# Down stage of a Strassen feed-forward: two sets of PSUM banks, left operands in three steps, the next rows' norm in half steps

## The chip, the cores and the metric

One core of one Trainium2 chip. The metric is the device time of one execution in microseconds, the median of three runs.

## What is computed

Rows `x` are 2 x 2048 rows of 1024 values, all float32. Cut to what matters, the reference is:

```python
x = x + attention(layernorm(x))            # one head of 256, then Wo and bo
n = layernorm(x)                           # no gain, no bias
h = relu(n @ up_w) ** 2                    # 1024 -> 2048
shared = h @ down_w                        # 2048 -> 1024
rw = sum of the two largest of n @ gate_w  # 8 gates
routed = ((n @ fc1_w) @ expert_w * rw) @ fc2_w      # 1024 -> 512 -> 512 -> 1024
x = x + layernorm(shared + routed) * ln_gamma + ln_beta
```

The change lies in the second product of the feed-forward, `h @ down_w` together with the routed part: the down stage.

## The kernel before

The attention comes first (lines 406 to 759) and writes its rows to DRAM (`x1`). Then the feed-forward runs over four pairs of row blocks (`for b in range(NBB)`, line 999). A pair is 2 x 512 rows. Each b has an up stage (line 1061) and a down stage (line 1165). Instructions of this part stand in the order in which they are written (`manual_schedule`, line 998); the attention ahead of it is ordered by a scheduler.

**Matmuls.** Every float32 operand is split into a high and a low half that the matmul can take (`hi` a copy, `lo` the difference). A product of two such operands is three matmuls (`Pass3`, line 117). A matmul here is 128x128 by 128x512 and fills one PSUM bank.

**Products.** Both stages use a Strassen-like scheme: seven products of quarters instead of eight. The down stage takes them in the order p1, p2, p6, p5, p3, p7, p4. A product has 10 pieces of the inner dimension (k, `NK`), and for each piece four row tiles (t, `NB`): 12 matmuls per k, 120 per product, 840 per stage. Each product sums its four row tiles in four banks (`accs`, line 1167). p2, p3 and p4 go on adding to the banks of the product before them (`a.more()`, line 1170), after that one's sums have been copied or added into `y` (lines 1212 to 1229: on ScalarE, called ACT, for p1 and p2, on VectorE, called DVE, for the others). `acc_bank` (line 840) hands out banks of two pools, `psb` (2 banks) and `psa` (4), in a rotation of six. The pool `psc` (2 banks) isn't used by the down stage.

**Right operands (w).** `next_piece` (line 827) keeps three pieces ready. In each call it ends one piece, starts loads until two are under way, and casts one. For a raw piece the cast is on ACT (line 813) and the difference on DVE (line 821). A finished piece is written to DRAM by the POOL queue (line 824, `w_p<-w`), so that later b load both halves at once (line 793). All loads of w are on the SP queue (lines 793 and 796). b=0 has all pieces raw and stores those of even i, b=1 has those of odd i raw and stores them, b=2 and b=3 only load. There are seven w buffers.

**Left operands (sp).** `cast_s` (line 1024) does the Strassen sum of h on DVE, where a product has one (p2 line 1035, p6 line 1029, p5 line 1033), and casts the result on ACT (line 1039). `end_s` (line 1042) takes the difference on DVE (line 1044), and for p6 one more (line 1046). `next_s` (line 1056) keeps two ready. So in the loop at piece k, the difference of piece k+1 is taken, and sum and cast of piece k+2 are issued. There are four sp buffers.

**The norm of the next rows.** `Norm.step` (line 922) works on four tiles of 128 rows of the next pair in a pipeline of 11 steps. A full step issues, in this order: a load of a tile (SP queue), the transpose of a normalised tile on DVE and its write to DRAM (lines 213 and 218, POOL queue, `xt_d<-xblk`), the normalisation of a tile (two small DVE operations, lines 276 and 282, then ACT, line 283), the second moment and the first moment of two tiles (ACT, lines 271 and 259), and the fetch of a transposed tile (line 224, POOL queue, `xt<-xt_d`). Tile t is loaded in step t and goes through first moment, second moment, normalisation, write and fetch 2, 3, 4, 5 and 7 steps later. `norm1` steps at k = 0, 2, 4, 6, 8 of p1 and p2 and at k=0 of p6; `norm2` likewise in p5, p3 and p7 (lines 1182 to 1184). b=3 has no next rows.

**Other work in the down stage.** In p7 and p4 the tiles of norm1 are split for the next up stage (line 1189), and `out_step` (line 974) finishes output rows: a load of `res` (SP), a transfer that adds beta (POOL), moments on ACT, two DVE operations (lines 966 and 967) and the write of the output (POOL).

Of the kernel before, what the change touches and what calls it, by code (L numbers as in the profile page):

```python
# [17 lines left out]
P = 128  # L18
SQ = 32
W = 512  # L20
# [5 lines left out]
def kernel(  # L26
# [33 lines left out]
    NB = W // P  # L60
# [777 lines left out]
    n_bank = [0]  # L838
# [74 lines left out]
    class Norm:  # L913
# [2 lines left out]
        STEPS = NB + 7  # L916

        def __init__(self, n):
            self.n, self.i = n, 0
            self.r, self.m, self.d, self.x = {}, {}, {}, {}  # L920

        def step(self):
            load, first, second, norm, write, fetch = (
                self.i - lag for lag in (0, 2, 3, 4, 5, 7)
            )
            self.i += 1
            if load in range(NB):
                self.r[load] = load_row(x1[self.n][ts(load, P), :])
            if write in range(NB):
                self.d[write] = transpose_write(self.r[write])  # L930
            if norm in range(NB):
                self.m[norm].normalise()
            if second in range(NB):
                self.m[second].second()
            if first in range(NB):
                self.m[first] = Moments(self.r[first], "n")
            if fetch in range(NB):
                self.x[fetch] = fetch_tile(self.d[fetch])

    class Out:  # L940

# [56 lines left out]
    with tc.manual_schedule():  # L998
        for b in range(NBB):
# [19 lines left out]
                "p1": "11", "p2": "12", "p6": None, "p5": "21", "p3": "12", "p7": "11", "p4": "22",  # L1019
            }  # L1020
            todo_s = DOWN[:]
            sp, sp_cast = [], []

            def cast_s(at=None):
                p, k = todo_s.pop(0)
                a11, a12, a21, a22 = (h_at(a, k) for a in ("11", "12", "21", "22"))
                if p == "p6":
                    v = half("s2")
                    add(v, a11, a22, ALU.add)
                else:  # L1030
                    v = h_at(FROM[p], k)
                if p == "p5":
                    add(a21, a21, a22, ALU.subtract)
                elif p == "p2":
                    add(a11, a11, a21, ALU.subtract)
                t = at
                if t is None:
                    t = wp.tile([P, 2 * W], FR, tag="sp", name="sp", bufs=4)
                nc.scalar.copy(t[:, 0:W], v)  # L1039
                sp_cast.append((v, t, a12 if p == "p6" else None))  # L1040

            def end_s():
                v, t, a12 = sp_cast.pop(0)
# [2 lines left out]
                    add(a12, a12, v, ALU.subtract)  # L1046
                sp.append(t)

            def more_s(n):
                while (todo_s or sp_cast) and len(sp) < n:  # L1050
                    if sp_cast:
                        end_s()
                    if todo_s and not sp_cast:
                        cast_s()

            def next_s():
                more_s(2)
                return sp.pop(0)

            rwb, acc = [None, None], {}  # L1060
            for m, (p, i) in enumerate(UP):
                flush()
                w = next_piece()
                if p != "p2":
                    acc[i] = Pass3(acc_bank("pu"), NCC // 2)
                ps = acc[i].ps
                if p == "p2":
                    acc[i].more()
                for c in range(NCC // 2):
                    acc[i].add(piece(w, c, P, slice(0, P)), piece(X[p], c, W, slice(0, W)))  # L1070
                lat, pair = i >= HU // P, i % 2 and i < HU // P
                c22, c21 = h_at("22", i), h_at("21", i) if m >= 2 * NK else None
                if p == "p1":
                    nc.scalar.copy(c22, ps)
                elif p == "p2":
                    if lat:
                        add(h_at("11", i), ps, rwb[0], ALU.mult)
                    else:
                        relu(h_at("11", i), ps)
                        if pair:  # L1080
                            square(h_at("11", i, 2))
                elif p == "p4":
                    nc.scalar.copy(c21, ps)
                elif p == "p6":
                    add(c22, ps, c22, ALU.subtract)
                    add(c21, c21, c22, ALU.subtract)
                elif p == "p5":
                    add(c22, c22, ps, ALU.add)
                elif p == "p3":
                    c12 = h_at("12", i)  # L1090
                    add(c12, c22, ps, ALU.add)  # L1091
                    if lat:
                        add(c12, c12, rwb[0], ALU.mult)
                    elif pair:
                        relu(h_at("12", i, 2), h_at("12", i, 2))
                        square(h_at("12", i, 2))
                else:
                    add(c21, c21, ps, ALU.add)
                    add(c22, c22, ps, ALU.subtract)
                    if lat:  # L1100
                        add(c21, c21, rwb[1], ALU.mult)
                        add(c22, c22, rwb[1], ALU.mult)
                    elif pair:
                        for v in ("21", "22"):
                            relu(h_at(v, i, 2), h_at(v, i, 2))
                            square(h_at(v, i, 2))

                if m % 2 and m < 15:
                    out_step()
                if b == 0 and m in (0, 1, 2, 4, 6, 8, 9, 10, 11, 12, 13):  # L1110
                    norm2.step()

                if m == 12:
                    x_t[1] = norm2.x
                    X["p4"] = new_x()
                if m >= 13 and m % 2 and m < 2 * NK:
                    split_x(x_t[1], 1, (m - 13) // 2, X["p4"], split_late)
                elif m >= 2 * NK and p != "p7":
                    n = {"p4": "p6", "p6": "p5", "p5": "p3", "p3": "p7"}[p]
                    if i == 1:  # L1120
                        X[n] = new_x()
                    if i % 2 and i < 2 * NB:
                        if p == "p4":
                            sums_x(x_t, i // 2)
                        r_, f_ = PLACE[n]
                        split_x(x_t[r_], f_, i // 2, X[n], split_late)

                if m == 0:
                    ga = half("ga")[: 2 * NE, :]
                    nc.scalar.copy(ga, gate_part(X["p1"], 0))  # L1130
                elif m == 2:
                    gs = half("gs")[: 2 * NE, :]
                    add(gs, ga, gate_part(X["p2"], 1), ALU.add)
                    gt = Gate(gs)
                elif (p, i) == ("p4", 1):
                    add(ga, ga, gate_part(X["p4"], 1), ALU.add)
                elif (p, i) == ("p7", 0):
                    add(ga, ga, gate_part(X["p7"], 0), ALU.subtract)
                    gt = Gate(ga)
                if m == 6 or (p, i) == ("p7", 3):  # L1140
                    gt.largest()
                elif m == 10 or (p, i) == ("p7", 6):
                    rwb[p == "p7"] = gt.spread()
                if p == "p7" and i >= NK - 5:
                    if sp_cast:
                        end_s()
                    if len(sp) < 3:
                        cast_s()
            X = {}


# [12 lines left out]
                norm1, norm2 = Norm(2 * b + 2), Norm(2 * b + 3)  # L1164
            for j, p in enumerate(("p1", "p2", "p6", "p5", "p3", "p7", "p4")):
                if p in ("p1", "p6", "p5", "p7"):
                    accs = [Pass3(acc_bank("pd"), NK) for _ in range(NB)]
                else:
                    for a in accs:
                        a.more()  # L1170
# [5 lines left out]
                for k in range(NK - late):  # L1176
# [2 lines left out]
                    for t in range(NB):  # L1179
                        down(t, s, w)  # L1180
                    if more:
                        for m, n in enumerate((norm1, norm2)):
                            if k % 2 == 0 and 3 * m <= j < 3 * m + 3 and n.i < Norm.STEPS:
                                n.step()
                        if j >= 5 and k % 2 and k < 2 * NB:
                            n = "p1" if j == 5 else "p2"
                            if k == 1:
                                X[n] = new_x()
                            split_x(norm1.x, j - 5, k // 2, X[n], split_late)
# [12 lines left out]
                if late:  # L1202
                    last_w = [next_piece() for _ in range(late)]
                    both = unit("last")
                    while len(sp) + len(sp_cast) < late:
                        if sp_cast:
                            end_s()
                        i = len(sp) - late + 2
                        cast_s(both[:, ts(i, 2 * W)] if i >= 0 else None)
                    end_s()  # L1210
                    last = [(sp.pop(0), w) for w in last_w]
                for t in range(NB):
                    for s, w in last if late else ():
# [74 lines left out]
```

## Time and profile before

| | us |
|---|---|
| median of 3 runs | 2413.64 (2413.22 to 2415.35) |
| the profiled execution's own time | 2414.37 |
| its span, first to last instruction | 2412.4 |
| TensorE busy | 2348.1 |
| VectorE (DVE) busy | 1463.5 |
| ScalarE (ACT) busy | 1131.3 |
| POOL busy | 299.5 |

The mean granted TensorE clock is 0.992 of full speed, and DMA moves 250 GB/s on the mean. In the profile, PE is the matmul side of TensorE and PEld its weight loads, which overlap. Matmuls overlap each other too, so a busy PE is not a PE at its peak: the distance from one start to the next tells more than the duration of one. An idle time is put down to the instruction that ended it. A share of busy time is a mean over stages with different limits, and is to be read by stage.

### The profile page before, as it was taken

What the parts mean: (1) busy time and instruction counts of PE and PEld (TensorE: products, weight loads), DVE (VectorE), ACT (ScalarE), POOL (GpSimd) and SP (SyncE); (2) the same over time, 40 slices, a digit from 0 to 9 for tenths busy, and PEclk for the clock granted to TensorE, in tenths of its full rate; (3) what the DMA queues carried; (4) which work ended last, traced back from release to release, by engine and by line L of the source; (5) the groups of instructions that cost most, each with busy time, mean ns of one, the idle gap of its engine ahead of it and who ended that gap; (6) DMA issues with size and microseconds to landing.
All of it is one profiled execution on the core that took longest, in us unless ns stands there. A gap on an engine that the chain in (4) does not pass through costs nothing.

```text
span 2412.4 us, 29279 instructions
## 1 busy us (share of the span) xinstructions
PE 2348.1 (97%) x10704; PEld 1922.9 (80%) x10704; DVE 1463.5 (61%) x2168; ACT 1131.3 (47%) x1846; POOL 299.5 (12%) x450
## 2 busy tenths in 40 slices
PE   8999899999998999999999999999999999999998
PEld 7888778888787778777777877777888887788886
DVE  5566549888777466687736458653446663445545
ACT  5555445555544553666552274544135354314224
POOL 3222110012110010011210011110000010000001
PEclk9999999999999999999999999999999999999999
DMA  5867883999996666677997778897557798655695
GB/s 186 320 245 266 286 201 110 287 317 320 285 244 183 214 230 184 230 244 243 337 307 237 239 265 316 316 333 259 194 184 266 257 325 292 212 194 185 203 310 189
DMA packets 225807, 603.99 MB, mean 250 GB/s; under 512 B 18768, under 2 KB 80720, under 8 KB 223616
## 3 DMA queue, kind: packets, MB, share of 16 engines
q1 hardware_dynamic: 152160, 334.02, 40.5%
q0 software_dynamic: 73504, 268.11, 36.3%
q8 instruction: 85, 1.39, 0.2%
q14 instruction: 58, 0.48, 0.1%
HBM read 448.96 MB, written 210.76 MB: 273 GB/s over the span
## 4 chain that ended last, share of the span: by engine, by line
PE 69%; issue 12%; DVE 6%; DMA 5%; ACT 5%; POOL 2%; POOLq 0%; SPq 0%; ACTq 0%; DVEq 0%
PE pu L130 28%; PE pd L130 21%; PE po L130 6%; PE ps L130 6%; PE pw L130 3%; DMA w<-wt 2%; DVE xblk L213 1%; DMA xres<-in_L_attn_bo_dram 1%; PE pg L870 1%; ACT xrow L283 1%; PE pf L130 1%; PE pq L130 1%; ACT junk L271 1%; DMA w_p<-w 1%; DVE w L821 1%
## 5 line engine op out<-in xcount | busy, mean ns | idle before, releaser
L130 PE MATMUL pd<-w,sp 128*128 128x512 f32 x3336 | 769.6, 392 | 18.8 <-DVE sp L1044 8.7
L130 PEld LDWEIGHTS pd<-w,sp 128*128 128x128 f32 x3336 | 625.8, 188 | 161.5 <-DVE sp L1044 18.0
L130 PE MATMUL pu<-xh,w 128*128 128x512 f32 x2240 | 692.9, 390 | 1.5 <-DVE w L821 0.8
L130 PEld LDWEIGHTS pu<-xh,w 128*128 128x128 f32 x2240 | 419.2, 188 | 92.4 <-DVE w L821 2.3
L130 PE MATMUL pu<-xl,w 128*128 128x512 f32 x1120 | 436.5, 390 | 2.9 <-DVE xl L150 2.8
L130 PEld LDWEIGHTS pu<-xl,w 128*128 128x128 f32 x1120 | 210.2, 188 | 48.3 <-DVE xl L150 4.6
L1044 DVE TENSOR_TENSOR sp<-h,sp 128x512 fp32r<-128x512 f32 x238 | 162.4, 687 | 128.2 <-ACT sp L1039 127.9
L1039 ACT CAST sp<-h 128x512 fp32r<-128x512 f32 x238 | 145.6, 618 | 182.7 <-PE pd L130 132.8
L130 PE MATMUL ps<-q,k 128*128 128x512 f32 x768 | 196.9, 394 | 3.7 <-DVE max L560 3.6
L130 PE MATMUL po<-p,v 128*128 128x512 f32 x768 | 197.2, 396 | 1.2 <-ACT p L142 1.1
L813 ACT CAST w<-w 128x512 fp32r<-128x512 f32 x210 | 128.1, 617 | 149.1 <-DMA w<-wt 140.3
L821 DVE TENSOR_TENSOR w<-w 128x512 fp32r<-128x512 f32 x210 | 142.8, 685 | 88.7 <-ACT w L813 87.0
L130 PEld LDWEIGHTS ps<-q,k 128*128 128x128 f32 x768 | 143.0, 189 | 38.5 <-DVE max L560 9.0
L130 PEld LDWEIGHTS po<-p,v 128*128 128x128 f32 x768 | 144.8, 190 | 31.9 <-ACT p L142 1.5
L824 POOL DMA_DIRECT2D w_p<-w x140 | 75.7, 541 | 586.6 <-DVE w L821 525.9
L992 ACT ACTIVATE h<-h 128x1024 f32<-128x1024 f32 x48 | 50.6, 1055 | 208.0 <-DVE h L1091 159.7
L555 ACT COPY s<-ps 128x512 f32<-128x512 f32 x128 | 75.0, 586 | 152.3 <-PE ps L130 148.9
L150 DVE TENSOR_TENSOR xl<-xt,xh 128x512 fp32r<-128x512 f32 x104 | 71.6, 688 | 120.8 <-ACT xh L149 120.7
L213 DVE STREAM_TRANSPOSE xblk<-xrow 128x1024 f32<-128x1024 f32 x60 | 120.4, 2007 | 39.1 <-ACT xrow L283 36.4
L560 DVE TENSOR_TENSOR max<-ps,max 128x512 f32<-128x512 f32 x120 | 82.4, 687 | 45.2 <-ACT s L555 45.1
L130 PE MATMUL pq<-xha,w_h 128*128 128x512 f32 x256 | 99.7, 389 | 0.0
L130 PE MATMUL pq<-xha,w_l 128*128 128x512 f32 x256 | 99.7, 389 | 0.0
(181 smaller groups left out, 3040.7 us busy)
## 6 DMA issues: line engine op xcount, KB each, us to landing
w<-w_p SPq DMA_DIRECT2D x350, 512.0 KB, 4.3
w_p<-w POOLq DMA_DIRECT2D x140, 512.0 KB, 4.7
w<-wt SPq DMA_DIRECT2D x210, 256.0 KB, 3.6
xt_d<-xblk POOLq DMA_DIRECT2D x56, 512.0 KB, 3.5
xt<-xt_d POOLq DMA_DIRECT2D x56, 512.0 KB, 6.3
wt<-in_L_ffn_up_w_dram POOLq DMA_DIRECT2D x9, 2048.0 KB, 24.9
wt<-in_L_ffn_down_w_dram POOLq DMA_DIRECT2D x9, 2048.0 KB, 34.1
xres<-in_L_attn_x_dram SPq DMA_DIRECT2D x32, 512.0 KB, 12.4
```

The costliest lines, as they stand in the source:

```text
L130: nc.tensor.matmul(self.ps, lhsT=a, rhs=b, start=self.i == 0, stop=self.i == self.n - 1, skip_group_check=self.on,)
L150: late_ops.append(lambda: nc.vector.tensor_tensor(lo, t, f32(hi), ALU.subtract))
L213: nc.vector.transpose(b.rearrange("p (q k i) -> p q k i", q=P // SQ, i=SQ), r.rearrange("p (k i q) -> p q k i", k=NCC, i=SQ),)
L271: nc.scalar.activation(self.junk(), self.v, AF.Square, bias=self.nm, accum_out=s2)
L555: nc.scalar.copy(s["s"][k // 4][:, ts(k % 4, W)], pm)
L560: nc.vector.tensor_tensor(s["max"], pm, s["max"], ALU.max)
L813: nc.scalar.copy(w[:, 0:W], f32(w)[:, W : 2 * W])
L821: nc.vector.tensor_tensor(w[:, W : 2 * W], v[:, W : 2 * W], v[:, 0:W], ALU.subtract)
L824: nc.gpsimd.dma_start(out=kept[key], in_=w.bitcast(FP))
L992: nc.scalar.activation(o, v, AF.Relu)
L1039: nc.scalar.copy(t[:, 0:W], v)
L1044: add(t[:, W : 2 * W], v, f32(t)[:, 0:W], ALU.subtract)
```

## The change

The down stage's banks: p1 with p2, and p5 with p3, take two banks of `psb` and two of `psc`; p6, and p7 with p4, take the four of `psa`. The rotation of `acc_bank` starts anew in each b. Left operands: sum, cast and difference are three steps, `sum_s`, `cast_s` and `end_s`, one k apart, so that at piece k the sum of k+3, the cast of k+2 and the difference of k+1 are issued. The norm: a step falls into two halves, load, transpose with its write and normalisation in the first, second and first moments and the fetch in the second. One half is issued after each of the k = 0 to 7 of p1, p2, p6 (norm1) and p5, p3, p7 (norm2), and none at k = 8 and 9. The number of instructions on ACT, DVE, POOL and SP is the same. SP's order is the same. On POOL, the write of the fourth transposed tile and the fetches of tiles 1 and 2 move from p2 to p6 and from p3 to p7, and the fetch of tile 3 moves from k=0 to k=5 of p6 and p7. On TensorE, the first six matmuls of the first up product now stand among the last ones of the attention.

```diff
-        def step(self):
+        def step(self, halves=(0, 1)):
             load, first, second, norm, write, fetch = (
                 self.i - lag for lag in (0, 2, 3, 4, 5, 7)
             )
-            self.i += 1
-            if load in range(NB):
...
+            if 0 in halves:
+                if load in range(NB):
+                    self.r[load] = load_row(x1[self.n][ts(load, P), :])
+                if write in range(NB):
+                    self.d[write] = transpose_write(self.r[write])
+                if norm in range(NB):
+                    self.m[norm].normalise()
+            if 1 in halves:
+                if second in range(NB):
+                    self.m[second].second()
+                if first in range(NB):
+                    self.m[first] = Moments(self.r[first], "n")
+                if fetch in range(NB):
+                    self.x[fetch] = fetch_tile(self.d[fetch])
+                self.i += 1
+
+        def half_step(self):
+            if self.i < Norm.STEPS:
+                self.step((self.half,))
+                self.half = 1 - self.half
...
-            def cast_s(at=None):
+            def sum_s():
                 p, k = todo_s.pop(0)
...
-                t = at
+                sp_sum.append((v, a12 if p == "p6" else None))
+
+            def cast_s(t=None):
+                v, a12 = sp_sum.pop(0)
                 if t is None:
                     t = wp.tile([P, 2 * W], FR, tag="sp", name="sp", bufs=4)
                 nc.scalar.copy(t[:, 0:W], v)
...
+            def step_s(at=None):
+                if sp_cast:
+                    end_s()
+                if sp_sum:
+                    cast_s(at)
+                if todo_s:
+                    sum_s()
+
             def more_s(n):
-                while (todo_s or sp_cast) and len(sp) < n:
-                    if sp_cast:
-                        end_s()
-                    if todo_s and not sp_cast:
-                        cast_s()
+                while (todo_s or sp_sum or sp_cast) and len(sp) < n:
+                    step_s()
...
+            n_bank[0] = 1
             for m, (p, i) in enumerate(UP):
...
                 if p in ("p1", "p6", "p5", "p7"):
-                    accs = [Pass3(acc_bank("pd"), NK) for _ in range(NB)]
+                    pools = (psb, psb, psc, psc) if p in ("p1", "p5") else (psa,) * 4
+                    accs = [Pass3(bank(q, "pd"), NK) for q in pools]
...
                     if more:
-                        for m, n in enumerate((norm1, norm2)):
-                            if k % 2 == 0 and 3 * m <= j < 3 * m + 3 and n.i < Norm.STEPS:
-                                n.step()
+                        if j < 6 and k < NK - 2:
+                            (norm1, norm2)[j // 3].half_step()
```

Two further places follow from the three steps: the end of the up stage calls `step_s` in each of its last five pieces, and the last product of b=3 prepares its five held-back pieces with `step_s`.

More of the change, by code (lines that the diff above doesn't have):

```diff
@@ L918, in __init__ @@
         def __init__(self, n):
-            self.n, self.i = n, 0
+            self.n, self.i, self.half = n, 0, 0
             self.r, self.m, self.d, self.x = {}, {}, {}, {}
-        def step(self):
+        def step(self, halves=(0, 1)):
             load, first, second, norm, write, fetch = (
@@ L925, in step @@
             )
-            self.i += 1
-            if load in range(NB):
[L928 to L938, printed above, removed]
+            if 0 in halves:
[17 more added lines that the diff above has]
+                self.half = 1 - self.half
     class Out:
@@ L1021 @@
             todo_s = DOWN[:]
-            sp, sp_cast = [], []
-            def cast_s(at=None):
+            sp_sum, sp_cast, sp = [], [], []
+            def sum_s():
                 p, k = todo_s.pop(0)
@@ L1039, in cast_s @@
                 nc.scalar.copy(t[:, 0:W], v)
-                sp_cast.append((v, t, a12 if p == "p6" else None))
+                sp_cast.append((v, t, a12))
             def end_s():
@@ L1144 @@
                 if p == "p7" and i >= NK - 5:
[L1145 to L1148, printed above, removed]
+                    step_s()
             X = {}
@@ L1204 @@
                     both = unit("last")
[L1205 to L1210, printed above, removed]
+                    while len(sp) < late:
+                        i = len(sp) + len(sp_cast) - late + 2
+                        step_s(both[:, ts(i, 2 * W)] if sp_sum and i >= 0 else None)
                     last = [(sp.pop(0), w) for w in last_w]
```

## Prediction

> **What bounds the kernel now.** I first cut the span into stages, since a mean over stages with different limits says nothing on this change. Rows are the four down stages (b = 0 to 3); columns: window, its length, busy time and count per engine, granted clock, DMA share, GB/s.
>
> ```profile
> core 0: us, PE busy (x) PEld busy (x) DVE busy (x) ACT busy (x) POOL busy (x), PEclk, DMA share, GB/s
> 1004.40:1209.90 205.50, 196.14 (x841) 157.39 (x840) 158.22 (x247) 126.47 (x236) 34.84 (x59) 0.99 0.81 275
> 1411.30:1615.90 204.60, 195.62 (x841) 157.77 (x840) 136.88 (x211) 108.31 (x200) 34.75 (x59) 0.99 0.91 320
> 1817.20:2009.00 191.80, 191.35 (x841) 157.21 (x840) 115.92 (x175) 89.77 (x164) 16.17 (x24) 1.00 0.83 288
> 2210.20:2400.70 190.50, 190.50 (x841) 157.48 (x840) 99.98 (x150) 64.85 (x117) 9.71 (x13) 1.00 0.71 235
> ```
>
> All do the same 840 matmuls. b=3 never waits: 190.5/840 = 0.2268 us each, 2.72 us per k (12 matmuls), 27.2 per product. TensorE bounds all four; what can go is the excess: 15.0 + 14.1 + 1.3 = 30.4 us. By products, the windows that aren't 27.2, here of b=0 (p2, p3, p7, p4), and p7 of b=2:
>
> ```profile
> 1034.40:1065.70 31.30, 29.96 (x120) 23.49 (x121) 26.89 (x41) 19.47 (x35) 7.11 (x12) 0.95 0.71 233
> 1120.10:1151.20 31.10, 28.69 (x122) 22.18 (x121) 23.48 (x35) 18.71 (x33) 7.09 (x12) 1.00 0.76 247
> 1151.20:1181.60 30.40, 27.95 (x121) 22.20 (x120) 21.69 (x34) 21.21 (x44) 8.12 (x12) 1.00 1.04 359
> 1181.60:1210.10 28.50, 27.73 (x120) 22.39 (x121) 21.91 (x34) 12.58 (x23) 3.75 (x7) 1.00 0.91 300
> 1954.70:1981.90 27.20, 27.20 (x122) 22.52 (x121) 16.70 (x25) 18.71 (x38) 4.76 (x7) 1.00 1.04 357
> ```
>
> Two kinds: in p2 and p3 no resource is full and DMA is at 0.7; in p7 the DMA share is 1. The matmul timeline says who was late (last bracket):
>
> ```profile
> 1034.45 16.02 PE L130 MATMUL pd<-w,sp 128*128 128x512 f32 x61 [2.44 <-ACT y L1217]
> 1054.76 73.68 PE L130 MATMUL pd<-w,sp 128*128 128x512 f32 x323 [0.97 <-DVE sp L1044]
> 1129.43 0.49 PE L130 MATMUL pd<-w,sp 128*128 128x512 f32 x1 [0.99 <-ACT sp L1039]
> 1181.60 5.92 PE L130 MATMUL pd<-w,sp 128*128 128x512 f32 x25 [1.59 <-ACT sp L1039]
> ```
>
> Summing starts beyond 0.2268 us: p1's end 4.29 (b=0), 1.76 (b=1); p2 from k4 2.37, 2.48, 0.12; p3 3.88, 2.16, 1.40: together **18.46**. p7 and p4: 1.46 + 3.05, 5.43 + 2.40, none: 12.34. Why p2 and p3 wait is in the two queues in one full norm step:
>
> ```profile
> 1042.10 0.69 DVE L821 TENSOR_TENSOR w<-w 128x512 fp32r<-128x512 f32 x1 [2.71 <-ACT w L813]
> 1043.91 1.99 DVE L213 STREAM_TRANSPOSE xblk<-xrow 128x1024 f32<-128x1024 f32 x1
> 1045.97 0.16 DVE L282 TENSOR_TENSOR nb<-nm,rs 128x1 f32<-128x1 f32 x1
> ...
> 1046.17 1.25 ACT L283 ACTIVATE xrow<-xrow,nb,rs 128x1024 f32<-128x1024 f32 x1 [2.54 <-DVE nb L282]
> 1041.46 0.60 ACT L813 CAST w<-w 128x512 fp32r<-128x512 f32 x1
> ```
>
> Each engine idles 2.5 us for the other. DVE needs 4.03 us from its w to nb; ACT from normalise (1037.58) through second and first to the cast of the next w (ends 1042.06) 4.5. That is one closed loop, 8.6 us (nb ends 1037.54 and 1046.13), for two k of 5.44.
>
> **What the Trainium skill says.** PSUM — Partial Sum Buffer, "PSUM bank collisions raise a hardware error": readers and matmuls are to be kept apart by bank. So p2, which adds to p1's banks, waits for the copies; the trace agrees (2.44 us). Same page, "Engine vs sequencer instructions": ScalarE and VectorE queues are strict FIFO; the loop above shows it. TensorE: Matmul & The Clock Gate, "Part 1": an idle stretch halves the clock for some 3.4 us; here at 1034.4, nine starts that were 0.43 us instead of 0.23, 1.7 of the 4.29. DMA: Bandwidth & Descriptors, "Issuing engines are not separate DMA queues": all transfers interleave on 16 engines; p7 agrees, its w loads take 7 to 10 us to land, against 2.6 to 3.4 in p3.
>
> **The change, part by part** (against the profiled execution, 2414.4 us, span 2412.4).
>
> *Half steps, p1's end.* Before, the step at k=8 puts normalise, second and first (3.9 us) ahead of ACT's casts and the four copies of p1. Now the last half is at k=7, and ACT has 2 x 1.04 us of casts in 5.44 us before the copies. Gain 6.05, the clock dip with it.
>
> *Half steps, p2 and p3.* After nb ACT does normalise (1.2) and one cast before DVE may go on: 1.9 + 4.0 = 5.9 us per two k. ACT's own sum is 4 casts x 0.52 + 1.15 + 1.46 + 1.28 = 6.0. Both exceed 5.44, so p2 of b=0 loses 0.5 per full step. I carried both queues through k by k, each instruction at the start-to-start time of the rows above (DVE 0.60, transpose 1.91, reciprocal and nb 0.27; ACT casts 0.52), each waiting for its source. p1's last copy ends 0.8 us into p2; ACT's two casts then end at 1.8, DVE's w and sp at 2.5, for a use at 5.44 (k2): 2.9 early. The same at k4, k5, k6, k7, k8: 2.1, 2.8, 1.4, 2.2, 0.9 early. Two bare k give 0.9 each back. p2 has three transposes instead of four. p3 has no sums (0.6 less per k on DVE): least 0.5. b=1 and b=2 have less to cast. Gain 2.37 + 2.48 + 0.12 + 7.44 = 12.41; I leave 0.5 for the thin places, so **18.0** in all. The cover is those 0.5 to 0.9 us; without it some 0.5 per late k returns.
>
> *Fourth transpose.* It moves to p6 k0 and p7 k0. p6 has DVE at 4 x 0.6 = 2.4 per k, plus 1.9 once: sp is then 1.9 us early at k2 and gains 0.3 per k. p7 k0: the evictions of p3 end 0.9 us into it, then w, sp, transpose, w, sp: ready at 5.3 for k2 at 5.44. Nothing, but barely: the lead built in p3 hides it, and if DVE comes later, all of its delay is lost once, 0.1 to 2 us. Queued behind on DVE are w and sp of the next k, then the low half of a split tile; ACT's casts don't wait for them.
>
> *Three-step operands.* The same adds, casts and subtractions, the add one k earlier, so ACT's cast no longer waits for an add of its own k (63.9 us of idle ACT in 30 waits, which p6 without any stall shows to be off the path). The four sp buffers hold as before: two ready, one cast, one in use. A sum of p6 lives a k longer, three of four half buffers; no norm scratch is asked for then, its last is at k5 of p2. I add nothing beyond the above; if the buffers were short, an add would wait a k, which the sp lead of 1.9 us hides in part: 0.8 us per time.
>
> *Bank sets.* Before, six banks went round, so a product's first two were free and its last two were those that the previous product's first two copies left 1.4 us and more earlier. No matmul in the waits stands for a DVE eviction. Nothing: the matmuls on t0 and t1 hide it. If DVE came late, the new sets would save that, 0.7 us per copy, which no row shows. p1 to p2, p5 to p3, p7 to p4 still share banks. Resetting the rotation lets six matmuls of the first up product be issued among the last attention ones, one of them in a 7.44 us idle of TensorE at the half clock: 0.2 to 0.45, I take **0.3**.
>
> *DMAs that move.* SP's order is unchanged. On POOL, per block, the fourth write of xt_d and the fetches of tiles 1 and 2 go from p3 into p7 (k0, k1, k3), the third fetch from k0 to k5. Behind them wait the stored pieces (w_p), whose landing frees buffers for the next loads, and the beta adds. (For norm1 they go from p2 to p6, where the share is 0.78 to 0.91: room.) 512 KB at p7's 359 GB/s are 1.46 us, so 4.4 us of DMA time come into a product that has none free. Pairing each load with its matmuls, the time from landing to use sinks to 7.0 us in p7 of b=0 and to 1.0 at k3 of p4 in b=2. But two of the three were issued at p3's end and landed 8 to 10 us later, already among the traffic of p7; the share was 0.7 to 0.95 just before. So only what becomes idle there is lost: I estimate 2 us per block, not shown by the trace. b=0 and b=1 already stall and pay it; b=2 pays what exceeds 1.0, say 0.5: **+4.5**. Bounds: 4.4 x 3 - 1.0 = +12.2; below nothing, -6, if w_p, no longer behind a fetch that waits 4 us for its write, frees loads sooner.
>
> Sum: 2414.4 - 18.0 - 0.3 + 4.5 = 2400.6; the median of the runs is 0.7 under the profiled one: **2399.9**. With 2 us either way on the gain and 4 on the DMAs, 2394 to 2405.
>
> **Rivals.**
> - *The moved DMAs cost all they can* (+12.2): 2407.6. For: b=2's 1.0 us. Against: part was there already. 0.17.
> - *The loop only moves*: half of the 18 stays since 5.9 to 6.0 still exceed 5.44: 2408.9. For: slack of 0.5. Against: k8 and k9 are bare. 0.10.
> - *p7 eases too* (-6): 2389.4. For: w_p waits less. Against: its DMA share is 1. 0.14.
> - *Slower*: loads in p7 fall a ring behind. Pieces land too late, ACT waits for w with the sp cast behind it, stored pieces leave later and free buffers later. It decides when p7 and p4 rise by over 18.3 us, 6.1 per block, more than the moved transfers' own 4.4; at 8 per block 2419.4. 0.04.
> - *It doesn't do what it says*: another wait at p1's end takes its place, 2413. 0.04.
>
> **The numbers.** Likeliest case 0.51. The range takes in the easing and the two dear cases, 2389 to 2409; the last two, and tails of the others, are left out. About 0.2% (4.8 us) is what a measurement can tell from no change. Faster: 0.51 + 0.14 + 0.12 of the first rival + 0.06 of the second = 0.83; slower 0.04; same 0.13.
>
> **What would show it.** p2 and p3 at 27.2 us in all blocks, no wait for ACT y L1217, no half clock near p1's end; DVE waits for ACT w in p2 well under 2.5 us. p7 + p4 of b=0 and b=1 at 61 and 64 us (58.9, 62.3 now), b=2 at 55. I am wrong if p2 or p3 keep stalls, or if b=2 stalls by several us in p4.

## The result, and the profile after

| | before | after |
|---|---|---|
| median, us (6 runs each) | 2413.2 (2410.0 to 2415.4) | 2394.66 (2394.2 to 2400.8) |
| the profiled execution's own time | 2414.37 | 2396.25 |
| its span | 2412.4 | 2394.2 |

The ratio is 0.9925 (95%: 0.9915 to 0.9935), some 18 us faster. The forecast was 2399.9, range 2389 to 2409.

First the same cut by stage, after the change (window, its length, busy time and count per engine, granted clock, DMA share, GB/s):

```profile
core 0: us, PE busy (x) PEld busy (x) DVE busy (x) ACT busy (x) POOL busy (x), PEclk, DMA share, GB/s
1001.40:1199.30 197.90, 193.69 (x842) 158.35 (x841) 157.65 (x247) 127.71 (x236) 34.77 (x59) 0.99 0.86 285
1400.50:1597.60 197.10, 193.22 (x842) 158.57 (x841) 136.97 (x211) 108.37 (x201) 34.72 (x59) 0.99 0.94 332
1798.80:1990.90 192.10, 190.91 (x841) 157.48 (x841) 116.44 (x177) 90.64 (x165) 16.14 (x24) 1.00 0.84 287
2192.20:2382.60 190.40, 190.40 (x841) 157.52 (x839) 99.95 (x150) 65.02 (x117) 9.66 (x13) 1.00 0.72 235
```

The busy times of DVE, ACT and POOL are what they were; only the lengths of b=0 and b=1 have changed, by 7.6 and 7.5 us; b=2 is 0.3 us longer. By products (p2, p3, p7, p4 of b=0, then p7 and p4 of b=2):

```profile
1028.90:1056.10 27.20, 27.20 (x121) 22.53 (x121) 25.45 (x41) 24.21 (x44) 5.03 (x9) 1.00 0.83 259
1110.50:1137.70 27.20, 27.20 (x121) 22.53 (x121) 22.04 (x36) 22.26 (x40) 5.03 (x9) 1.00 0.81 257
1137.70:1169.00 31.30, 29.43 (x121) 23.33 (x120) 23.25 (x35) 20.49 (x42) 10.17 (x15) 0.95 1.02 343
1169.00:1199.30 30.30, 27.97 (x121) 22.45 (x122) 22.14 (x34) 13.22 (x25) 3.74 (x7) 1.00 0.93 310
1934.80:1962.00 27.20, 27.20 (x121) 22.52 (x121) 18.49 (x26) 18.71 (x38) 6.61 (x9) 1.00 1.00 327
1962.00:1990.90 28.90, 27.71 (x121) 22.34 (x121) 15.91 (x24) 6.43 (x11) 1.95 (x3) 1.00 0.95 341
```

p2 and p3 are at 27.2, the time of a product without a wait. p7 and p4 of b=0 have got longer (30.4 and 28.5 before), and p4 of b=2 waits for the first time. The matmul timeline of b=0 and of b=2 shows the same; a long piece is many matmuls without an idle time between them, and the bracket is the idle time before a piece with what ended it:

```profile
1001.43 161.31 PE L130 MATMUL pd<-w,sp 128*128 128x512 f32 x709
1164.56 10.43 PE L130 MATMUL pd<-w,sp 128*128 128x512 f32 x36 [1.81 <-DVE sp L1055]
1175.72 5.73 PE L130 MATMUL pd<-w,sp 128*128 128x512 f32 x24 [0.73 <-DVE sp L1055]
1183.02 16.43 PE L130 MATMUL pd<-w,sp 128*128 128x512 f32 x71 [1.56 <-DVE sp L1055]
...
1798.84 166.08 PE L130 MATMUL pd<-w,sp 128*128 128x512 f32 x732
1965.50 5.71 PE L130 MATMUL pd<-w,sp 128*128 128x512 f32 x24 [0.57 <-DMA w<-w_p]
1971.82 19.29 PE L130 MATMUL pd<-w,sp 128*128 128x512 f32 x84 [0.61 <-DMA w<-w_p]
```

In b=0, 709 matmuls, from p1 to p7's k=9, go without a wait that this view keeps apart; the wait for the copies of p1 is gone, and the half clock with it. In b=2 the matmuls now wait for a load itself (`DMA w<-w_p`).

Last, the loop that the prediction put the stalls down to, in p2 of b=0 after the change. These are two normalisations in a row on ACT with what lies between them, and the DVE operation that each waits for:

```profile
1042.33 0.16 DVE L282 TENSOR_TENSOR nb<-nm,rs 128x1 f32<-128x1 f32 x1
1048.27 0.16 DVE L282 TENSOR_TENSOR nb<-nm,rs 128x1 f32<-128x1 f32 x1
...
1042.58 1.24 ACT L283 ACTIVATE xrow<-xrow,nb,rs 128x1024 f32<-128x1024 f32 x1
1043.72 0.60 ACT L813 CAST w<-w 128x512 fp32r<-128x512 f32 x1
1048.46 1.25 ACT L283 ACTIVATE xrow<-xrow,nb,rs 128x1024 f32<-128x1024 f32 x1 [1.11 <-DVE nb L282]
```

nb ends at 1042.49 and 1048.43: one turn takes 5.9 us, as worked out, against 8.6 before. The cast of the next w follows the normalisation at once, and no longer behind two moments. A turn of 5.9 us is still longer than the 5.44 us of two k; what it is late by comes out of the lead that ACT and DVE have from elsewhere.

### The profile page after: what moved, and what is told of

Read it like the earlier page. It is cut to its first block, busy times and chain, and to the rows that moved or that the text cites. A ratio compares the mean times of both kernels' runs of the same rounds, so it can differ in the third digit from the quotient of the medians.

```text
span 2394.2 us, 29276 instructions
## 1 busy us (share of the span) xinstructions
PE 2341.5 (98%) x10704; PEld 1924.4 (80%) x10704; DVE 1461.7 (61%) x2168; ACT 1133.1 (47%) x1846; POOL 297.9 (12%) x450
## 4 chain that ended last, share of the span: by engine, by line
PE 78%; issue 9%; DMA 5%; DVE 3%; ACT 3%; POOL 2%; SPq 0%; POOLq 0%; DVEq 0%; ACTq 0%
PE pu L130 30%; PE pd L130 26%; PE ps L130 7%; PE po L130 7%; PE pw L130 3%; PE pg L870 1%; DMA w<-wt 1%; PE pf L130 1%; DMA xt<-xt_d 1%; PE pq L130 1%; DMA w<-w_p 1%; DMA w_p<-w 1%; DVE xblk L213 1%; PE psum L617 1%; ACT xrow L283 1%
```

## The experiments

Each comparison has its own runs of the kernel before on the same chip (medians 2411.4 to 2413.2). The two columns on the right are the stalls of the profiled execution: what the matmuls' starts lie apart beyond 0.2267 us, summed over p1 to p3 (that is p1, p2, p6, p5, p3) of all b, and over p7 and p4 by b. They are those of one execution each; the three kernels without half steps and without moved transfers (before, e2, e3) agree within 1 us in each column.

| kernel | median | ratio (95%) | p1 to p3 | p7 and p4: b=0, 1, 2 |
|---|---|---|---|---|
| before | 2413.2 | | 18.7 | 4.5, 7.8, 0 |
| after | 2394.7 | 0.9925 (0.9915 to 0.9935) | 0.3 | 7.1, 6.7, 1.7 |
| e1 half steps alone | 2397.0 | 0.9943 (0.9920 to 0.9965) | 0.3 | 6.3, 7.0, 1.7 |
| e2 three-step operands alone | 2410.9 | 0.9996 (0.9988 to 1.0005) | 18.1 | 4.1, 8.5, 0 |
| e3 banks alone | 2411.1 | 0.9996 (0.9987 to 1.0005) | 19.0 | 4.0, 8.8, 0 |
| e4 whole steps, none at the end | 2420.1 | 1.0031 (1.0021 to 1.0042) | 20.8 | 7.5, 11.6, 2.5 |
| e5 half steps to the end | 2396.1 | 0.9934 (0.9919 to 0.9949) | 4.6 | 5.6, 7.0, 0 |
| e6 norm2 early | 2386.0 | 0.9891 (0.9877 to 0.9906) | 1.5 | 1.4, 4.0, 0 |
| e7 output steps spread | 2395.2 | 0.9922 (0.9905 to 0.9938) | 0.3 | 3.7, 7.2, 0 |
| e8 early and spread | 2387.3 | 0.9897 (0.9882 to 0.9912) | 0.3 | 0, 4.6, 0 |
| e9 two more writes | 2405.5 | 0.9971 (0.9957 to 0.9984) | 0.3 | 8.4, 8.3, 7.7 |
| e10 early, outputs in the middle | 2388.8 | 0.9895 (0.9880 to 0.9910) | 0.3 | 1.9, 0.6, 1.3 |
| e11 early, outputs late | 2386.7 | 0.9887 (0.9873 to 0.9902) | 0.3 | 0, 1.4, 0 |
| e12 early, outputs in the middle for b = 0 to 2 | 2381.8 | 0.9881 (0.9864 to 0.9897) | 0.3 | 0.7, 0.8, 0 |

**e1: the half steps alone.** Banks and left operands as before.

```diff
 # the kernel before, with step and half_step as in the change
 ...
-                        for m, n in enumerate((norm1, norm2)):
-                            if k % 2 == 0 and 3 * m <= j < 3 * m + 3 and n.i < Norm.STEPS:
-                                n.step()
+                        if j < 6 and k < NK - 2:
+                            (norm1, norm2)[j // 3].half_step()
```

> The kernel before with the norm's half steps alone (none at k = 8 and 9), bank rotation and two-step left operands as before. My theory (the half steps open the loop between ACT and DVE, and that is all of the gain): about 2395, within 3 us of the changed kernel's 2394.7; p1 to p3 at 27.2 us in b = 0 to 2. Rival (the three-step operands open the loop, since ACT's cast no longer waits for a sum of its own k): most of the 18 us stays, 2405 to 2413. Rival (bank sets): the same, with the wait for the copies of p1 still there.

Measured 2396.98, with p1 to p3 of b = 0 to 2 free of stalls. So the half steps alone bring the gain, as far as these runs tell: the two medians are 2.3 us apart, and the intervals of the two ratios overlap.

**e2: the left operands in three steps alone.**

> The kernel before with the left operands in three steps alone. My theory: no difference, 2413 within 2.5 us, p2 of b=0 still at some 31 us. Rival (three steps open the loop): 2395 to 2403, p2 and p3 near 27.2.

Measured 2410.92, no difference from before (0.04%, with an interval of some 0.1% to either side). Its timeline in b=0 has the waits where they were:

```profile
1030.09 8.69 PE L130 MATMUL pd<-w,sp 128*128 128x512 f32 x37 [1.68 <-ACT y L1219]
1043.05 3.02 PE L130 MATMUL pd<-w,sp 128*128 128x512 f32 x12 [0.98 <-DVE sp L1047]
1125.08 0.49 PE L130 MATMUL pd<-w,sp 128*128 128x512 f32 x1 [0.97 <-ACT sp L1042]
```

The cast no longer waits for a sum of its own k, but it still stands behind normalise and two moments: the wait that was taken away was not the one that came last.

**e3: the two sets of banks and the restarted rotation alone.**

```diff
 # the kernel before
-                    accs = [Pass3(acc_bank("pd"), NK) for _ in range(NB)]
+                    pools = (psb, psb, psc, psc) if p in ("p1", "p5") else (psa,) * 4
+                    accs = [Pass3(bank(q, "pd"), NK) for q in pools]
...
+            n_bank[0] = 1
```

> The kernel before with the two sets of banks and the restarted rotation alone. My theory: 0 to 1 us faster, from the up matmuls that are issued in TensorE's idle time at the end of the attention; the down stages as before. Rival (banks held the matmuls up at the products' ends): p1's end loses its wait for the copies, 6 us faster or more, 2407.

Measured 2411.08. The wait for the copies of p1 is 2.2 us in b=0 and 2.5 in b=1, as large as without the sets: p1 and p2 share their banks either way. The matmuls issued early at the attention's end bring nothing that can be told: from the attention's last score matmul to the first matmul of the down stage of b=0 it takes 271.4, 272.5 and 272.4 us in the three profiles without them (before, e1, e2), and 271.6 and 272.5 in e3 and the changed kernel.

**e4: whole steps, none at a product's end.**

```diff
 # the changed kernel
-                        if j < 6 and k < NK - 2:
-                            (norm1, norm2)[j // 3].half_step()
+                        if j < 6 and k < NK - 2 and k % 2 == 0:
+                            n = (norm1, norm2)[j // 3]
+                            if n.i < Norm.STEPS:
+                                n.step()
```

> The changed kernel with whole norm steps at k = 0, 2, 4, 6, so none at a product's end, but not halved. My theory (halving opens the loop): the 6 us of p1's end are kept, the stalls inside p2 and p3 (12.4 us) come back for the greater part, with the moved transfers' cost in p7 and p4 as in the changed kernel: 2402 to 2408. Rival (what matters is only that no step is at a product's end): 2395.

Measured 2420.07, slower than before, which neither theory foresaw. Its matmul timeline in p1 and p2 of b=0:

```profile
998.91 38.77 PE L130 MATMUL pd<-w,sp 128*128 128x512 f32 x169
1038.00 2.79 PE L130 MATMUL pd<-w,sp 128*128 128x512 f32 x11 [0.31 <-DVE sp L1055]
1041.79 0.50 PE L130 MATMUL pd<-w,sp 128*128 128x512 f32 x1 [1.01 <-ACT sp L1050]
1042.60 3.01 PE L130 MATMUL pd<-w,sp 128*128 128x512 f32 x12 [0.30 <-DVE sp L1055]
1046.59 3.02 PE L130 MATMUL pd<-w,sp 128*128 128x512 f32 x12 [0.97 <-DVE sp L1055]
1049.92 3.01 PE L130 MATMUL pd<-w,sp 128*128 128x512 f32 x12 [0.31 <-DVE sp L1055]
1053.91 71.03 PE L130 MATMUL pd<-w,sp 128*128 128x512 f32 x312 [0.98 <-DVE sp L1055]
```

The first 169 matmuls pass over p1's end without a wait, so that part came as expected. But the loop inside p2 takes back what was won: p1 to p3 stall by 20.8 us against 18.7. Two causes fit, and no run sets them apart. A wait at p1's end gives ACT and DVE time to get ahead, and without it the same loop, too slow for its two k, runs out of lead in p2. And with four steps to a product in place of five, one step's work moves on: p2 of b=0 holds four normalisations here, three before. The changed kernel has those four as well and doesn't stall in p2, so what e4 shows against it is the halving. The rest is in p7 and p4 (21.6 against 12.3). They have the transfers of the changed kernel, which stalls there by 15.5; where the other 6 us come from is not shown.

**e5: half steps up to the end.**

```diff
 # the changed kernel
-                        if j < 6 and k < NK - 2:
+                        if j < 6:
```

> The changed kernel with a half step after every k, so five steps per product as before the change, the last half at k = 9. The transfers of norm2 lie again where they were before the change. My theory (the moved transfers cost 3 us in p7 and p4, most clearly 1.7 in b=2; halving opens the loop): b=2 loses its stall in p4, b=0 and b=1 are near 4.5 and 7.8 there; p1's end stalls again by 1 to 3 us in b=0 and b=1, since second and first stand ahead of the four copies; 2393 to 2398. Rival (the moved transfers cost nothing, the stalls of p7 and p4 only vary from run to run): p4 of b=2 keeps a stall near 1.7.

Measured 2396.13. p1's end stalls by 1.95 and 2.03 us:

```profile
1031.37 128.76 PE L130 MATMUL pd<-w,sp 128*128 128x512 f32 x565 [1.66 <-ACT y L1230]
```

p4 of b=2 has no stall, so the 1.7 us there, which are waits for a load, come from the moved transfers. What the free ends win (4 us) and what the moved transfers lose (1.6 in b=0, 1.7 in b=2) nearly cancel, and the medians of e5 and of the changed kernel are within 1.5 us.

**e6: norm2 early.** Its half steps follow norm1's directly, and none is left for p7.

```diff
 # the changed kernel
-                        if j < 6 and k < NK - 2:
-                            (norm1, norm2)[j // 3].half_step()
+                        if j < 5 and k < NK - 1:
+                            (norm1 if norm1.i < Norm.STEPS else norm2).half_step()
```

> The changed kernel with norm2's half steps directly behind norm1's, both at k = 0 to 8 of p1, p2, p6, p5, p3; none in p7. My theory (p7 and p4 are bound by DMA in b=0 and b=1, 512 KB costs 1.46 us there): four transfers of 512 KB per block leave p7, 5.8 us of DMA time; b=2 loses its 1.7, b=0 and b=1 lose 3 to 5 of about 7 each: 2384 to 2390. Rival (ACT and DVE are what is short in p7): p7 and p4 keep 5 us and more in b=0 and b=1, 2391 to 2395. Rival (earlier loads and p6's fuller DMA cost as much): 2395 or more.

Measured 2385.95, 11 us faster than e1 and 9 faster than the changed kernel. p7 and p4 of b=0 and of b=1:

```profile
1136.00:1163.20 27.20, 27.20 (x122) 22.32 (x120) 21.39 (x34) 20.92 (x43) 7.34 (x11) 1.00 0.97 299
1163.20:1191.70 28.50, 27.79 (x122) 22.42 (x122) 21.93 (x34) 12.93 (x24) 3.74 (x7) 1.00 0.96 324
1529.90:1560.40 30.50, 27.65 (x122) 22.23 (x120) 18.60 (x29) 18.31 (x38) 6.97 (x11) 1.00 1.04 347
1560.40:1588.20 27.80, 27.62 (x120) 22.51 (x121) 19.02 (x29) 10.96 (x21) 3.56 (x7) 1.00 0.97 338
```

In b=0 the DMA share of p7 is now just under 1 and p7 is at 27.2. In b=1, which loads both halves of every other piece and writes the rest, it is still over 1. Twelve transfers left p7 in the three blocks, and the stalls of p7 and p4 sank by 10.2 us. The step takes two more things out of p7: a transpose of 1.9 us on DVE, and the place that the transfers had on the POOL queue ahead of others. So e6 shows that norm2 costs time in p7, and not by itself that DMA time is the reason.

**e7: the output steps spread** over p7 and p4, at every third k; the same bytes in both together.

```diff
 # the changed kernel
-                    if j == 5 and k % 2 == 0 or j == 6 and k in (0, 2):
+                    if j >= 5 and (NK * (j - 5) + k) % 3 == 0 and NK * (j - 5) + k <= 18:
```

> The changed kernel with the seven output steps at every third k of p7 and p4 in place of every second k. The bytes of p7 and p4 together stay. My theory (DMA is full over both products in b=0 and b=1): b=2 loses its 1.7, b=0 and b=1 gain little, 2391 to 2395. Rival (ACT's moments, in a cluster ahead of the sp casts, are what stalls): b=0 and b=1 lose most of their 14 us, 2385 or less.

Measured 2395.15: no gain over the changed kernel. The 1.7 of b=2 are gone and b=0 falls from 7.1 to 3.7; b=1 keeps 7.2, now in one wait of 4.2 us at p4's first matmul and the half clock after it. There the step at k=9 has put DVE's output operations (2.5 us) ahead of those that take p7's sums into `y`, which the matmul waits for. The stalls sank by 4.6 and the median did not follow. The reason is at the end of the program: b=3 has only five k of p4 in this loop, so the steps at its k=5 and k=8 were never issued there, and two output tiles were finished after the last matmul. From the start of the last matmul to the end of the span it takes 17.2 us in e7 and 11.8 in the changed kernel. The last two writes of the output, on POOL, in the changed kernel and in e7:

```profile
2386.37 0.53 POOL L976 DMA_DIRECT2D out_dram<-y  x1 [2.87 <-DVE y L975]
2389.51 0.53 POOL L976 DMA_DIRECT2D out_dram<-y  x1 [2.61 <-DVE y L975]
```

```profile
2387.82 0.53 POOL L976 DMA_DIRECT2D out_dram<-y  x1 [2.04 <-DVE y L975]
2390.39 0.53 POOL L976 DMA_DIRECT2D out_dram<-y  x1 [2.04 <-DVE y L975]
```

The last matmul of e7 starts at 2378.0, 4.4 us before that of the changed kernel (2382.4); its last write is issued 0.9 us after.

**e8: both.**

> Both of these: norm2 out of p7, and the output steps at every third k. My theory: the two add up where DMA is short, 2382 to 2388. Rival: no better than norm2 out of p7 alone.

Measured 2387.26, no better than e6 alone, as the rival had it: b=0 is free, b=1 keeps 4.6, and the tail is 17.2 us as in e7.

**e9: two more writes in p7.**

```diff
 # the changed kernel, in the branch for b = 0 to 2
+                        if j == 5 and k in (2, 4):
+                            nc.gpsimd.dma_start(out=scratch[k // 2 - 1], in_=gamma_sb)
```

> The changed kernel with two more writes of 512 KB to DRAM (the gain vector's tile to a scratch tensor that nothing reads) on the POOL queue, at k = 2 and 4 of p7 in b = 0 to 2. They wait for nothing. My theory (p7 and p4 are full of DMA, 1.46 us per 512 KB): b=2 stalls by 1.7 + 2.9 = 4.6, b=0 and b=1 by 0 to 3 more: 2398 to 2403. Rival (DMA time is free there, and the queues' order is what stalls): within 1.5 us of the changed kernel.

Measured 2405.54, some 11 us slower than the changed kernel and more than my theory put. The matmul timeline of its b=2 (`issue` means that the view names nothing that ended the wait):

```profile
1804.90 163.45 PE L130 MATMUL pd<-w,sp 128*128 128x512 f32 x720
1972.35 14.13 PE L130 MATMUL pd<-w,sp 128*128 128x512 f32 x49 [3.99 <-issue]
```

p7 and p4 stall by 24.4 us against 15.5: 8.9 us for six transfers, 1.48 each, where 512 KB at the 359 GB/s of p7 take 1.46. Nothing else was added, and nothing waits for these writes, so added bytes alone cost this much. The agreement to 0.02 is no proof of the price of one transfer: the blocks share it unevenly (1.2, 1.7 and 6.0), and some of it isn't waiting. In each of the three blocks the clock was halved for 6.8 us at p4's start, against 3.4 us in b=0 and b=1, and none in b=2, of the changed kernel.

How the bytes cost time the traces show best in b=2, and there it isn't through the loads of w. The loads issued during p7, on the SP queue, took 7.9, 8.8 and 12.7 us to land on the mean (b=0, 1, 2), and 8.7, 9.3 and 12.9 in the changed kernel. What landed later are the transfers that stand behind the added writes on the POOL queue. The first two beta additions to `res` in b=2 took 14.4 and 21.0 us, against 10.2 and 14.6. DVE waits for them in the second output operation (L975), 13.7 us in p7 and p4 of b=2 against 3.3. Behind that operation, in DVE's queue, are the next difference of sp and the four operations that take p7's sums into `y` (L1243), and p4's first matmul, which goes on adding to p7's banks, has to wait for the first of these:

```profile
1969.76 1.28 DVE L975 SCALAR_TENSOR_TENSOR y<-y,rs,res 128x1024 f32<-128x1024 f32 x1 [4.50 <-DMA res<-in_L_ffn_ln_beta_dram]
1970.97 0.68 DVE L1056 TENSOR_TENSOR sp<-h,sp 128x512 fp32r<-128x512 f32 x1
1971.57 2.47 DVE L1243 TENSOR_TENSOR y<-y,pd 128x512 f32<-128x512 f32 x4
```

The first of the four ends at about 1972.3, and the matmul starts at 1972.35. So of the rival only one half falls: the added bytes weren't free. Its other half, that the order of the queues is what stalls, is what b=2 shows. The same writes on a queue without `res` would set the two apart; that wasn't run.

**e10 and e11: what is left of p7.** Both have norm2 early as in e6. e10 has the output steps away from the product's end, e11 puts them out of p7 for b = 0 to 2.

```diff
 # e10
-                    if j == 5 and k % 2 == 0 or j == 6 and k in (0, 2):
+                    if j == 5 and k in (0, 3, 6) or j == 6 and k in (0, 2, 4, 6):
 # e11
-                    if j == 5 and k % 2 == 0 or j == 6 and k in (0, 2):
+                    if j == 6 and k % 2 == 0 or not more and j == 5 and k % 2 == 0:
```

> norm2 out of p7 as in the kernel with the early norm, and the seven output steps at k = 0, 3, 6 of p7 and k = 0, 2, 4, 6 of p4, so none at a product's end. My theory: b=0 and b=2 without stalls, and the wait at k=0 of p4 in b=1 (3.1 us with a step at k=9) falls to 2 or less, since ACT's and DVE's queues are short at p7's end: 2381 to 2385. Rival (b=1 is short of DMA whatever the order): 3 us and more stay in b=1, 2385 to 2388.

> norm2 out of p7, and in b = 0 to 2 no output step in p7: five in p4, the rest in the next up stage, where the DMA share is 0.66 to 0.79. My theory: p7 is free of stalls in all blocks, and what is left is at most 2 us in p4 of b=1: 2380 to 2384. Rival (y and res hold their buffers longer, and the up stage waits for them): up stages longer than 201.0 us, 2386 or more.

Measured 2388.83 and 2386.67, both above what my theories put. In e10, b=1 is down to 0.6 us from e8's 4.6; in p7 the two differ by the step at k=9 alone, so it was the step at the product's end that held p4 up. Yet b=0 and b=2 stall by 1 us at p4's k=8, and the step at k=6 of p4 is one that b=3 never issues: its tail is 14.4 us. In e11 p7 is free in all blocks, and the rival's wait has come: the up stage of b=1 takes 205.7 us in place of 201.0. The waits of the matmuls in it:

```profile
PE pu L130 <- ACT h L1091: 2.8, 1, 2.8
```

That wait and the half clock after it (3.4 us from 1232.5) are in this stage alone. Whether the longer-held buffers are its cause wasn't tried.

**e12: the two lessons together.** norm2 early, the output steps of b = 0 to 2 away from p7's end and from p4's last k, those of b=3 where they were.

```diff
 # e6
-                    if j == 5 and k % 2 == 0 or j == 6 and k in (0, 2):
+                    if more and (j == 5 and k in (0, 3, 6) or j == 6 and k in (0, 2, 4)):
+                        out_step()
+                    if not more and (j == 5 and k % 2 == 0 or j == 6 and k in (0, 2)):
                         out_step()
```

> norm2 early, output steps in b = 0 to 2 at k = 0, 3, 6 of p7 and k = 0, 2, 4 of p4 (the seventh falls to the next up stage's first), in b=3 as in the changed kernel. e7, e8 and e10 moved b=3's steps too, and its p4 has only five k in the loop, so one or two steps came after the last matmul: from the last matmul's start to the end 17.2, 17.2 and 14.4 us, against 11.8 in the changed kernel. My theory (that tail is why the medians did not follow the stalls): 11.8 us of tail, 1 to 3 us of stalls in p7 and p4 together, median 2381 to 2384, faster than e6's 2386.0. Rival (the tail is no cause): 2386 to 2389 again.

Measured 2381.81, the lowest median of all, 29.6 us below before in its own comparison (e6: 25.6; the intervals of their ratios overlap). The tail is 11.9 us. p7 of b=0 and of b=1:

```profile
1137.70:1164.90 27.20, 27.20 (x122) 22.53 (x121) 17.54 (x29) 18.92 (x37) 4.49 (x7) 1.00 0.92 285
1530.00:1557.20 27.20, 27.20 (x121) 22.52 (x120) 13.82 (x23) 14.35 (x29) 4.50 (x7) 1.00 1.01 347
```

Both are at 27.2, b=1 with the DMA share still at 1. A full DMA share, then, is not yet a stall. Against e6 two things differ, fewer output transfers in p7 and no step near its end; which of them freed b=1 is set apart only by e8 and e10, and there it was the end.

## Why the prediction was right, point by point

**Half steps (18.0 of 18.46 predicted).** All 18.46 us went, and e1 shows that the half steps alone do it. The 0.3 us left in the table lie in p1's k=2 of b=0, and the kernel before has most of them too. The thin places, for which 0.5 was left, held: no stall in p2, p6 or p3 of any block. The turn of the loop was foreseen as 5.9 to 6.0 us and took 5.9. The rival that half would stay, since 5.9 is over 5.44, fell, because the lead covers the rest. That the two bare k at a product's end are needed for it e5 shows: with half steps there too, 4.6 us of stalls come back, most of them at p1's end. One reading was loose: of the nine starts at 0.43 us at p1's end the trace has six, and two others that are late; together they are the 1.7 us that was put.

**Three-step operands and banks (nothing).** Right for both (e2, e3), each within 0.1% of before. The 0.3 for the early up matmuls was within what can't be told.

**Fourth transpose (nothing).** Right: p6 is at 27.2 in every block, and the "barely" at k=2 of p7 didn't show: p7's first stall of more than 0.2 us in b=0 is at k=9.

**Moved transfers (+4.5 predicted; +3.2 measured).** The sum was near, in part by luck, for its parts were less so: +2.6 in b=0, -1.2 in b=1 and +1.7 in b=2, where 2, 2 and 0.5 were put. e5, with the transfers back at their places, gives 5.6, 7.0 and 0 beside 7.1, 6.7 and 1.7: so they cost 1.6 and 1.7 in b=0 and b=2 and nothing in b=1. In b=2 the backlog came to 2.7 us (1.7 of stall after 1.0 of lead), not 2; the time from landing to use at k=3 of p4 fell from 1.01 us to 0.13. In b=1 the kernels without half steps show 7.8, 8.5 and 8.8 (before, e2, e3) and those with them 6.7 to 7.0 (the changed kernel, e1, e5), wherever the transfers stand; so something in the half steps helps there, and what it is stays open. In b=0 the other microsecond (4.5 to 5.6) appears without any moved transfer. A reason that fits, but that no run sets apart: p3's stalls gave the loads of p7 a lead (14.8 us from landing to use at p7's k=0 before, 13.1 after), and that went with them.

The mechanism was right for b=2, where the matmuls wait for a load of w, and in part another in b=0 and b=1. There the ten loads of p7 took 5.3 and 7.0 us to land on the mean, less than before (6.5 and 8.6). What lands later is `res`. The prediction names the beta additions behind the moved transfers on the POOL queue, but puts no cost on them. They took 11.8 to 18.8 us, against 7.2 to 9.5 before and 6.5 to 10.3 in e5. DVE's second output operation waits for them 2.7 and 5.9 us in p7 and p4 of b=0 and b=1, and not at all before or in e5. In p4 of b=0 such a wait stands ahead of the sp that ends the matmuls' wait of 1.56 us at 1183.02:

```profile
1180.47 1.28 DVE L975 SCALAR_TENSOR_TENSOR y<-y,rs,res 128x1024 f32<-128x1024 f32 x1 [1.74 <-DMA res<-in_L_ffn_ln_beta_dram]
1181.68 0.68 DVE L821 TENSOR_TENSOR w<-w 128x512 fp32r<-128x512 f32 x1
1182.28 0.69 DVE L1055 TENSOR_TENSOR sp<-h,sp 128x512 fp32r<-128x512 f32 x1
```

How much of the stalls in b=0 and b=1 is due to `res`, and how much to ACT's waits for the loads of w that b=0 and b=1 cast, no run sets apart.

**What the sum lacked.** The forecast lies 5.2 us above the median. In the two profiled executions the down stages account, by the starts of their matmuls, for 15.2 us of the 18.1 (13.8 were forecast for everything). The other 3.0 lie before the first down stage, in the attention, which the change leaves as it was. The matmul timeline of the kernel before has there:

```profile
640.76 2.01 PE L130 MATMUL ps<-q,k 128*128 128x512 f32 x6 [1.80 <-DVE max L560]
```

with the clock halved for 3.4 us from 641.9. The profile of the changed kernel and the twelve of the experiments have no half clock there, whether they hold the change's parts or not. Matched matmul by matmul, the kernel before and the changed one are level to 0.3 us up to there and 4.1 us apart after it; 1.1 us go back at the end of the attention, where the changed kernel's clock is halved for longer (13.7 us against 10.2). Over the fourteen profiles the first down stage starts between 998.4 and 1004.7 us, though of the change only the restarted rotation and the last five pieces of the up stage lie before it. So this is a difference between executions and no part of the change; the profile on which the forecast was built was one of the longer ones. How often it occurs in the timed runs isn't known. The gain that the stages show is 15 us; that the medians differ by 18 is in part that wait, and how much remains open.

## What to carry to other kernels

Where two in-order engines feed each other, count the turn of the loop between them, not their busy shares: here DVE was 86% and ACT 62% busy in p2 of b=0, and one turn took 8.6 us where 5.4 were to be had. Cutting the long run of instructions between two links of the loop (half steps) brought the turn to 5.9, near enough for the lead to cover the rest; moving the run to another place (e4), or taking away a wait that wasn't the last (e2, e3), did not. And follow each moved step with its transfers to the stage where they land, and to what stands behind them on their queue there. In p7, with its DMA share of 1, the moved transfers cost time, in part through the `res` transfers behind them, so the better schedule is the one that ends before that stage (e6), with no long step at the end of a product (e12).

## What the runs showed of the hardware that was not expected

With the DMA share at 1, six added writes of 512 KB that no instruction waits for made the matmuls 8.9 us later in all (e9); by their bytes, at 359 GB/s, they take 8.8. The delay wasn't spread over all traffic: the loads of w on the SP queue landed no later (12.7 us on the mean in b=2, 12.9 without the writes), while the `res` transfers behind the writes on the POOL queue took up to 21.0 us, against 14.6. And the half clock came after shorter waits than expected. The Trainium skill, "TensorE: Matmul & The Clock Gate", Part 1, puts the drop after an idle window of about 3.4 us; the measurement differs and decides: in the down stages of the fourteen profiles here, no matmul that started up to 1.9 us late was followed by it, and each that started 1.96 us late or more was, by 3.4 us of half clock up to 2.9 us, and by 6.8 us from 4.0 to 4.2 us (3.4 in one case at 4.1).
